# r of blocks 1 to 3 as seven products over pairs of chunks, with a new layout of PSUM

## The chip, the cores and the metric

The kernel runs on one core of one Trainium2 chip. The metric is the device time of one execution in microseconds (us), the median of several runs. A profile of one execution gives every instruction's start and duration on the engines: TensorE (PE, with its weight loads as PEld), VectorE (DVE), ScalarE (ACT), GpSimd (POOL), and SyncE (SP), which issues most DMAs.

## What is computed

One layer over 2048 tokens of 512 channels, all in float32. `xn` is the layer norm of x, and the result is x plus an attention and a feed-forward part:

```python
rvk = einsum('btc,dc->btd', xn, W_rvk)        # 512 -> 3 x 512
r, v, k = split(rvk, 3)
y = sigmoid(r) * wkv(time_decay, time_first, k, v)    # a recurrence over the tokens
attn = einsum('btc,dc->btd', y, W_out)
...
idx = top_k(softmax(xn @ classifier_w.T) + bias, 2)   # of 12: 8 experts, 4 that return x
act = silu(xn @ gate_w[e].T) * (xn @ up_w[e].T)
ffn = sum over the two of weight * (act @ down_w[e].T)
```

## The kernel before

**Tiles.** Channels are cut into 4 chunks of 128, tokens into 4 blocks of 512. A unit is one block and one chunk, 16 units in all, numbered 0 to 15 in order of block and chunk. k, v and r of a unit are 128 channels by 512 tokens. The feed-forward part works on 23 tiles of 128 gathered rows, each with one expert (tiles at places 3 and 7 mix two).

**The products of a unit.** `project` (L273) makes k, v and r of units 0 and 1 plainly: four matmuls of 512 columns each. `seven` (L393) makes units 2 to 15: k and v together are a 2 x 2 block product (halves of the input channels by halves of the tokens), done with seven products in place of eight, by sums of token halves (S1 to S4, `sum_tokens`) and of weights (`wsum`). Each product is two matmuls of 256 columns (L408). Results are added up within PSUM: products 1, 6, 7 and 4 add into one bank in turn and ScalarE copies the sum out after each; 5 and 3 share another bank; 2 has its own. VectorE adds the last parts (`add`, L418); those adds are "owed" and emitted some steps later. r stays plain in `seven`: four matmuls of 512 (L421), and ScalarE takes exp(-r) straight from PSUM (L464). `seven` is a generator of 11 steps.

**The scan of a unit** (`scan`, L296) is the recurrence on VectorE, in five stages: first L307 to L314, then two exponentials on ScalarE (L316, L317), then L323 to L334 (scan steps, and 1 + exp(-r) at L333), then a reciprocal of the first half (L337), then that of the second half and the product y (L340).

**The attention's output** (`attention`, L1012) takes y: a row of 128 tokens is four matmuls of 512 columns (L1040) into a bank `pw`. For rows 0 to 11 VectorE then evicts it with one operation (L1052); rows 12 to 15 are added to rows read back (L1049, L1036).

**A tile of the feed-forward part** is `first_half` (up products into `pg` by `up`, L903, `activate` with ScalarE's tanh at L915 and VectorE at L916 and L917, a gather) and `second_half` (`unite` and `flip`, ScalarE copies for the transposes; `finish` of the tile before, down products into `po`, L851, that ScalarE evicts at L935; fetches).

**PSUM** is eight banks in four pools of two: `ps_mm`, `ps_gu`, `ps_o` and `ps_tr`. `pg` is in `ps_gu`, `po` in `ps_o`, p1 and p3 of `seven` in `ps_mm`, r and p2 in `ps_tr`. Attention rows 0 to 5 take `ps_gu` (even rows) and `ps_o` (odd rows); rows 6 to 11 `ps_o` (even) and `ps_mm` (odd); rows 12 and 13 `ps_o`, 14 and 15 `ps_mm`.

**What sets the order.** Every engine runs its instructions in the order in which the program emits them. The head (norms, transposes, routing) is written out by hand, with `fill(n)` putting n steps of the products between; 50 steps are done there. Behind the head a table (L1094 on) gives every piece of work a due time in a unit of its own and emits the pieces in order of it:

```python
total = groups * 3.43 + TILES * 5.2
one = total / groups / CC                       # a slot: one step or one row's matmul
plan((u - 1) * UNIT + 9 + at, stages[u])        # at = 0, 5, 7.5, 12, 14: five stages of a scan
plan((CC * m + k) * one, group)                 # group m: four steps of products, or a row
plan(CC * (m + 1) * one + 1, group)             # the eviction of that row
plan(4 + spread * i, first_half, i, TILES)      # spread = (total - 12) / TILES
plan(4 + spread * (i + 0.6), second_half, i, TILES)
```

`after` says which groups are rows 0 to 7 of the attention; rows 8 to 15 follow the table. A tile of a pool takes a buffer whose last reader has been emitted, and its first writer waits on the chip until that reader is done.

## Time and profile before

| | us |
|---|---|
| median of 3 runs | 368.78 (368.5 to 370.45) |
| the profiled execution | 368.04, of which its span is 366.3 |
| busy in it: TensorE | 360.8 |
| VectorE | 298.5 |
| ScalarE | 149.0 |
| GpSimd | 88.0 |

The granted TensorE clock is 1.0 throughout. In a line of the timeline the first number is the start in us, the second the duration, then engine, source line, operation, what is written and read, shapes, how many instructions are merged, and in brackets the idle time of the engine before it and what ended it. A float32 matmul leaves two records. [...] The costliest groups of TensorE are the up products (L903, 78.8 us), r (L421, 53.9), the attention's output (L1040, 53.7), the down products (L851, 39.5) and the seven products (L408, four groups of 29.1, 28.9, 28.8 and 14.4).

### The profile page before, as it was taken

The page shows a single profiled execution, that of the slowest core. Times are in us where ns is not written, and L with a number is a line of the kernel's source. Part 1 is how long each engine was busy: PE and PEld are TensorE (multiplying, and loading weights), DVE is VectorE, ACT ScalarE, POOL GpSimd, SP SyncE. Part 2 cuts the span into 40 slices and gives each one's busy share as a digit, 9 for nine tenths or more (in the row PEclk, how much of TensorE's full clock was granted, in tenths as well). Part 3 has the DMA queues.
Part 4 walks back from the last instruction along what each step waited for, and adds up shares of the span by engine and source line. Part 5 has one row for each costly group of instructions (what it writes and reads, how often), then busy time and mean ns, then how long its engine had stood idle before and what let it go on. Part 6 is the DMA issues. An engine that isn't in the chain of part 4 may idle for free. (4 is left out here: it accounts for less than half of the span.)

```text
span 366.3 us, 5027 instructions
## 1 busy us (share of the span) xinstructions
PE 360.8 (99%) x1752; PEld 241.6 (66%) x1752; DVE 298.5 (82%) x508; ACT 149.0 (41%) x267; POOL 88.0 (24%) x120
## 2 busy tenths in 40 slices
PE   8999999999999999999999999999999999999996
PEld 3555468788755686466767777877766787764444
DVE  5888999989998576999597957699969498869971
ACT  2676122345454525255433463435453526332000
POOL 6000200321221232243212214333313222122130
PEclk9999999999999999999999999999999999999999
DMA  7999940886777999979997669999769996924782
GB/s 265 405 350 364 346 145 14 314 262 178 181 218 232 315 332 229 263 152 263 372 361 201 127 204 260 247 234 244 217 208 278 256 244 91 351 41 58 174 137 93
DMA packets 47131, 84.44 MB, mean 231 GB/s; under 512 B 26496, under 2 KB 26880, under 8 KB 43328
## 3 DMA queue, kind: packets, MB, share of 16 engines
q1 hardware_dynamic: 39792, 64.05, 54.9%
q0 software_dynamic: 7312, 20.06, 25.6%
q8 instruction: 14, 0.23, 0.3%
q14 instruction: 13, 0.11, 0.1%
HBM read 63.25 MB, written 19.27 MB: 225 GB/s over the span
## 5 line engine op out<-in xcount | busy, mean ns | idle before, releaser
L903 PEld LDWEIGHTS pg<-xgT,gw 128*128 128x128 f32 x672 | 78.4, 192 | 5.9 <-issue 4.9
L903 PE MATMUL pg<-xgT,gw 128*128 128x128 f32 x672 | 78.8, 275 | 0.2 <-DMA gw<-in_gu_dram 0.2
L939 POOL DMA_INDIRECT out_dram<-yo,to_i x23 | 39.0, 1697 | 149.4 <-DMA out_dram<-yo,to_i 45.6
L337 DVE RECIPROCAL sums<-sums 128x256 f32<-128x256 f32 x32 | 54.6, 1729 | 0.0
L421 PE MATMUL pr<-xnT,wrvk 128*128 128x512 f32 x112 | 53.9, 594 | 0.0
L1040 PE MATMUL pw<-wout_sb,yT 128*128 128x512 f32 x120 | 53.7, 593 | 0.1
L1040 PEld LDWEIGHTS pw<-wout_sb,yT 128*128 128x128 f32 x120 | 22.5, 190 | 26.9 <-issue 26.8
L851 PE MATMUL po<-dw,act 128*128 128x512 f32 x84 | 39.5, 592 | 0.0
L915 ACT ACTIVATE act<-pg 128x256 f32<-128x256 f32 x23 | 8.8, 383 | 69.1 <-PE pg L903 62.6
L916 DVE SCALAR_TENSOR_TENSOR act<-act,pg 128x256 f32<-128x256 f32 x23 | 9.6, 418 | 33.4 <-ACT act L915 33.2
L809 POOL DMA_INDIRECT xg<-xs,token_i x23 | 25.5, 1108 | 46.1 <-DVE empty L760 25.2
L421 PEld LDWEIGHTS pr<-xnT,wrvk 128*128 128x128 f32 x112 | 20.4, 190 | 15.1 <-issue 13.3
L408 PE MATMUL p<-xnT,wrvk 128*128 128x256 f32 x112 | 29.1, 382 | 0.1
L408 PE MATMUL p<-S,wrvk 128*128 128x256 f32 x112 | 28.9, 380 | 0.0
L408 PE MATMUL p<-S,T 128*128 128x256 f32 x112 | 28.8, 379 | 0.0
L323 DVE TENSOR_TENSOR_SCAN sums<-obv,state,a 128x512 f32<-128x512 f32 x16 | 20.5, 1281 | 9.4 <-ACT obv L317 9.3
L408 PEld LDWEIGHTS p<-S,T 128*128 128x128 f32 x112 | 21.0, 190 | 8.7 <-issue 6.2
L851 PEld LDWEIGHTS po<-dw,act 128*128 128x128 f32 x84 | 16.0, 190 | 16.2 <-issue 15.1
L884 ACT COPY xgT<-xq 128x1024 uint16<-128x1024 uint16 x22 | 25.5, 1159 | 0.0
L408 PEld LDWEIGHTS p<-xnT,wrvk 128*128 128x128 f32 x112 | 20.8, 190 | 6.8 <-issue 2.9
L408 PEld LDWEIGHTS p<-S,wrvk 128*128 128x128 f32 x112 | 21.0, 190 | 4.4 <-issue 1.8
L876 ACT COPY xp<-xg 128x1024 uint16<-128x1024 uint16 x22 | 23.0, 1047 | 0.5 <-DMA xg<-xs,token_i 0.5
(224 smaller groups left out, 487.2 us busy)
## 6 DMA issues: line engine op xcount, KB each, us to landing
gw<-in_gu_dram SPq DMA_DIRECT2D x25, 1024.0 KB, 7.9
dw<-in_down_dram SPq DMA_DIRECT2D x25, 512.0 KB, 5.5
x<-in_x_dram SPq DMA_DIRECT2D x16, 256.0 KB, 5.4
xs<-x SPq DMA_DIRECT2D x16, 256.0 KB, 4.4
wrvk<-in_w_rvk_dram SPq DMA_DIRECT2D x3, 1024.0 KB, 8.2
xrow<-xs SPq DMA_DIRECT2D x8, 256.0 KB, 6.4
out_dram<-xrow POOLq DMA_DIRECT2D x8, 256.0 KB, 7.0
xrows<-xs SPq DMA_DIRECT2D x8, 256.0 KB, 7.9
```

What stands on the lines that cost most here:

```text
L323: nc.vector.tensor_tensor_scan(sq, bs, a2, s[:, 3:4], ALU.add, ALU.mult)
L337: nc.vector.reciprocal(den[:, hs], den[:, hs])
L408: nc.tensor.matmul(ps[:, :HALF], w[:, k, cs], a[:, k, :], start=(begin and k == 0), stop=(end and k == 1), skip_group_check=True,)
L421: nc.tensor.matmul(pr, wrvk_sb[0][:, k, cs], xnT[b][:, k, :], start=(k == 0), stop=(k == CC - 1))
L809: nc.gpsimd.indirect_dma_start(out=xg, out_offset=None, in_=xs, in_offset=bass.IndirectOffsetOnAxis(ap=token[:, column(i) : column(i) + 1] ...
L851: nc.tensor.matmul(out_, lhs[:, c, :], rhs[0][:, c, :], start=(c == 0), stop=(c == last))
L876: nc.scalar.copy(xp, st[i]["xg"].bitcast(U16).rearrange("p (c h) -> p h c", h=2))
L884: nc.scalar.copy(xgT.bitcast(U16).rearrange("p c (t h) -> p c t h", h=2), st[i]["xq"].rearrange("p (h c) t -> p c t h", h=2),)
L903: nc.tensor.matmul(pg[:, c // IC, c % IC * P : (c % IC + 1) * P], w[0][:, k, rs], xgT[:, k, :], start=(k == 0), stop=(k == CC - 1),)
L916: nc.vector.scalar_tensor_tensor(act, act, 1.0, pg[:, 0, :], ALU.add, ALU.mult)
L939: nc.gpsimd.indirect_dma_start(out=out, out_offset=bass.IndirectOffsetOnAxis(ap=index, axis=0), in_=yo[ps], in_offset=None, compute_op=ALU ...
L1040: nc.tensor.matmul(po, yT[b][:, c, j * P : (j + 1) * P], wout_sb[:, c, :], start=(c == 0), stop=(c == CC - 1),)
```

## The change

Units 2 and 3 of block 0 still go through `seven`. For blocks 1 to 3 a new generator, `pair`, takes two chunks at once. k and v of each chunk go by the seven products as before (A and B), and r of the two chunks together (R) is now a 2 x 2 block product too, halves of the input channels by halves of the tokens for the two chunks, done with seven products; the token sums are shared with k and v. A pair is 21 steps of one product each in a fixed order. Four sums of r's weights are made, three into new tiles and one in place of the weights: four VectorE operations of 512 elements (`sum_r_weights`), emitted behind the head's last `turn(0)`. exp(-r) is now a ScalarE operation in place, emitted in the scan's third stage. The owed adds carry a clock: each is emitted two steps after its product.

PSUM is laid out anew when the first pair begins (`change_banks`): `ps_o` stays with two buffers; p1 has two, p2, p3, pr (both halves of r's sums) and gu one each. Attention rows 0 to 5 are all in `ps_o`; the later rows that were in `ps_mm` are in p1, the last half row in p3, the rest in `ps_o` as before. The two transposes of mixed tiles (`turn_act`) move from `ps_gu` to `ps_o`.

The plan changes with the number of steps (178 to 172): `groups` 40 to 39, `UNIT` 17.4 to 17.05, rows 4 to 7 one group earlier. The pool of r gets six buffers in place of four, and the memory for the descriptors of GpSimd's DMAs is set to 8192 bytes.

```diff
-    erp = pool("er", 4)
+    erp = pool("er", 6)
...
-    ps_mm = pool("ps_mm", 2, space=bass.MemoryType.PSUM)
-    ps_gu = pool("ps_gu", 2, space=bass.MemoryType.PSUM)
-    ps_o = pool("ps_o", 2, space=bass.MemoryType.PSUM)
-    ps_tr = pool("ps_tr", 2, space=bass.MemoryType.PSUM)
+    ps_o = pool("ps_o", 2, **psum)
+    early = ExitStack()
+    ps_mm, ps_gu, ps_tr = (
+        early.enter_context(tc.tile_pool(name=name, bufs=2, **psum)) for name in ("ps_mm", "ps_gu", "ps_tr")
+    )
+    banks = {}
+
+    def change_banks():
+        early.close()
+        for name, n in (("p1", 2), ("p2", 1), ("p3", 1), ("pr", 1), ("gu", 1)):
+            banks[name] = pool(f"ps_{name}", n, **psum)
...
         er = kvr[b, c, "r"]
+        if b > 0:
+            nc.scalar.activation(er, er, AF.Exp, scale=-1.0)
...
+    def sum_r_weights():
+        for n in (2, 3, 4):
+            rsum[n] = sump.tile([P, 2, 2, P], F32, tag=f"R{n}", name=f"R{n}")
+        nc.vector.tensor_sub(rsum[3], r_weights(1, 1), r_weights(0, 1))
+        nc.vector.tensor_add(rsum[2], rsum[3], r_weights(0, 0))
+        nc.vector.tensor_sub(rsum[4], r_weights(1, 0), rsum[2])
+        rsum[1] = r_weights(0, 1)
+        nc.vector.tensor_sub(rsum[1], r_weights(0, 1), r_weights(0, 0))
...
+        def m1():
+            src = multiply(1)
+            nc.scalar.copy(place(pool_, *k_at, "k")[:, :HALF], src)
...
+        def m2():
+            src = multiply(2)
+            owe(lambda: nc.vector.tensor_add(t["k"][:, :HALF], t["k"][:, :HALF], src))
...
+        def m3():
+            src = multiply(3)
+            nc.scalar.copy(t["more"][:, :HALF], src)
+            owe(lambda: nc.vector.tensor_add(t["v"], t["v"], t["more"]))
...
+    def pair(b, c):
+
+        A, _ = sevens(b, c, False)
+        B, next_sums = sevens(b, c + 1, False)
+        R, _ = sevens(b, c, True)
+        order = "A1 A5 R1 A6 A2 R5 A7 A3 R6 A4 B1 R2 B5 B6 R7 B3 B7 R3 B2 B4 R4".split()
+        done = set()
+        for name in order:
+            while owed and owed[0][0] <= clock[0]:
+                owed.pop(0)[1]()
+            {"A": A, "B": B, "R": R}[name[0]][int(name[1])]()
...
+    def owe(work):
+        owed.append((clock[0] + 2, work))
...
-        for u in range(LEAD, len(units)):
+        for u in range(LEAD, CC):
             yield from seven(*units[u])
+        change_banks()
+        for b in range(1, NTB):
+            for c in range(0, CC, 2):
+                yield from pair(b, c)
...
-            st[i]["pg"] = ps_gu.tile([P, 2, INTER], F32, tag="gu", name=f"pg{i}")
+            st[i]["pg"] = bank("gu", f"pg{i}", (2, INTER))
...
-            if i < (NTB - 2) * NJ - 2 and j % 2 == 0:
-                po = ps_gu.tile([P, C], F32, tag="gu", name=f"pw{i}")
-            elif i < (NTB - 2) * NJ - 2:
-                po = ps_o.tile([P, C], F32, tag="o", name=f"pw{i}")
-            elif j >= 2 if i in orows else j % 2 == 1:
-                po = ps_mm.tile([P, C], F32, tag="mm", name=f"pw{i}")
+            if i >= (NTB - 2) * NJ - 2 and (j >= 2 if i in orows else j % 2 == 1):
+                po = bank("p1", f"pw{i}")
             else:
                 po = ps_o.tile([P, C], F32, tag="o", name=f"pw{i}")
...
-    STEPS = 2 * 3 * CC + 11 * (len(units) - LEAD)
+    STEPS = 2 * 3 * CC + 11 * (CC - LEAD) + 21 * (len(units) - CC) // 2
...
-    UNIT = 17.4
-    after = {10: (0, 0), 11: (0, 1), 16: (0, 2), 17: (0, 3), 30: (1, 0), 31: (1, 1), 38: (1, 2), 39: (1, 3)}
-    groups = (STEPS - DONE) // CC + len(after)
+    UNIT = 17.05
+    after = {10: (0, 0), 11: (0, 1), 16: (0, 2), 17: (0, 3), 29: (1, 0), 30: (1, 1), 37: (1, 2), 38: (1, 3)}
+    groups = -(-(STEPS - DONE) // CC) + len(after)
...
-    nc = bacc.Bacc("TRN2", target_bir_lowering=False, num_devices=1)
+    nc = bacc.Bacc("TRN2", target_bir_lowering=False, num_devices=1, dynamic_dma_scratch_size=8192)
```

More of the change, by code (lines that the diff above doesn't have):

```diff
@@ L82, in layer, with bank @@
     dram = pool("dram", 1, space=bass.MemoryType.DRAM)
-    ps_mm = pool("ps_mm", 2, space=bass.MemoryType.PSUM)
-    ps_gu = pool("ps_gu", 2, space=bass.MemoryType.PSUM)
-    ps_o = pool("ps_o", 2, space=bass.MemoryType.PSUM)
-    ps_tr = pool("ps_tr", 2, space=bass.MemoryType.PSUM)
+    psum = dict(space=bass.MemoryType.PSUM)
+    ps_o = pool("ps_o", 2, **psum)
[8 more added lines that the diff above has]
+            banks[name] = pool(f"ps_{name}", n, **psum)
+    def bank(name, label, shape=(TB,)):
+        return banks[name].tile([P, *shape], F32, tag=name, name=label)
     routing = ExitStack()
@@ L362, in sum_first_weights, with r_weights @@
         nc.vector.tensor_sub(wsum[1], weights(1, 0), weights(2, 0))
+    rsum = {}
+    def r_weights(k, n):
+        both = wrvk_sb[0][:, 2 * k : 2 * k + 2, :].rearrange("p k (q w n) -> p k q w n", q=2, w=2)
+        return both[:, :, :, 1 - n, :]
+    def sum_r_weights():
[6 more added lines that the diff above has]
+        nc.vector.tensor_sub(rsum[1], r_weights(0, 1), r_weights(0, 0))
     def part(b, k, t):
@@ L391, in factors, with r_factors @@
         }[n]()
+    def r_factors(b, n):
+        w = {
+            1: lambda: r_weights(0, 0),
+            2: lambda: r_weights(1, 0),
+            3: lambda: r_weights(1, 1),
+            4: lambda: rsum[4],
+            5: lambda: rsum[1],
+            6: lambda: rsum[2],
+            7: lambda: rsum[3],
+        }[n]()
+        return factors(b, n)[0], w
     def seven(b, c):
@@ L427, in next_sums @@
                 for m in ns:
-                    owed.append(lambda m=m: sum_tokens(b + 1, m))
+                    owe(lambda m=m: sum_tokens(b + 1, m))
         p1 = bank(ps_mm, "mm", "p1_")
@@ L451, in seven @@
         multiply(p2, 2, True, True)
-        owed.append(lambda: add(k[:, :HALF], p2[:, :HALF]))
+        owe(lambda: add(k[:, :HALF], p2[:, :HALF]))
         next_sums((1, 2))
@@ L470, in seven, with sevens, place, at @@
         nc.scalar.copy(more[:, :HALF], p3[:, :HALF])
-        owed.append(lambda: add(v, more))
+        owe(lambda: add(v, more))
         next_sums((4,))
         yield
+    def sevens(b, c, with_r):
+        n = f"{b}_{c}"
+        t, ps = {}, {}
+        def place(pool_, name, c_, role):
+            t[role] = kvr[b, c_, name] = pool_.tile([P, TB], F32, tag=name, name=f"{name}{b}_{c_}")
+            return t[role]
+        def at(m):
+            which = {2: "p2", 3: "p3", 5: "p3"}.get(m, "p1")
+            if with_r and which != "p2":
+                ps.setdefault("pr", None)
+                if ps["pr"] is None:
+                    ps["pr"] = bank("pr", f"pr{n}")
+                h = which == "p3"
+                return ps["pr"][:, h * HALF : (h + 1) * HALF]
+            if m in (1, 2, 5):
+                ps[which] = bank(which, f"{which}{'r' if with_r else ''}_{n}")
+            return ps[which][:, :HALF]
+        def multiply(m):
+            dst = at(m)
+            if with_r:
+                a, w = r_factors(b, m)
+                rows_ = lambda k: w[:, k, c // 2, :]
+            else:
+                a, w = factors(b, m)
+                rows_ = lambda k: w[:, k, c * P : (c + 1) * P]
+            first = m in (1, 2) or (m == 5 and not with_r)
+            for k in range(2):
+                nc.tensor.matmul(
+                    dst,
+                    rows_(k),
+                    a[:, k, :],
+                    start=(first and k == 0),
+                    stop=(k == 1),
+                    skip_group_check=True,
+                )
+            return dst
+        def next_sums(*ns):
+            if c == CC - 1 and b + 1 < NTB:
+                for m in ns:
+                    owe(lambda m=m: sum_tokens(b + 1, m))
+        pool_, k_at, v_at = (erp, ("r", c + 1), ("r", c)) if with_r else (kvp, ("k", c), ("v", c))
+        def m1():
+            src = multiply(1)
+            nc.scalar.copy(place(pool_, *k_at, "k")[:, :HALF], src)
+        def m6():
+            src = multiply(6)
+            nc.scalar.copy(place(pool_, *v_at, "v")[:, :HALF], src)
+        def m5():
+            src = multiply(5)
+            t["more"] = five.tile([P, TB], F32, tag="more", name=f"more{'r' if with_r else ''}{n}")
+            nc.scalar.copy(t["more"][:, HALF:], src)
+        def m2():
+            src = multiply(2)
+            owe(lambda: nc.vector.tensor_add(t["k"][:, :HALF], t["k"][:, :HALF], src))
+        def m7():
+            src = multiply(7)
+            nc.scalar.copy(t["v"][:, HALF:], src)
+        def m4():
+            src = multiply(4)
+            nc.scalar.copy(t["k"][:, HALF:], src)
+        def m3():
+            src = multiply(3)
+            nc.scalar.copy(t["more"][:, :HALF], src)
+            owe(lambda: nc.vector.tensor_add(t["v"], t["v"], t["more"]))
+        return {1: m1, 2: m2, 3: m3, 4: m4, 5: m5, 6: m6, 7: m7}, next_sums
@@ new lines, in pair @@
+    def pair(b, c):
[8 more added lines that the diff above has]
+            {"A": A, "B": B, "R": R}[name[0]][int(name[1])]()
+            done.add(name)
+            for m, users in ((1, "B5 R5"), (2, "B6 R6"), (3, "B7 R7"), (4, "B3 R3")):
+                if name in users and set(users.split()) <= done:
+                    next_sums(m)
+            clock[0] += 1
+            yield
@@ L475, in emit_owed @@
+    clock = [0]
+    def owe(work):
+        owed.append((clock[0] + 2, work))
     def emit_owed(force=False):
         while owed and (force or not head):
-            owed.pop(0)()
+            owed.pop(0)[1]()
     head = True
@@ L503, in emit @@
         for _ in range(n):
-            owed.pop(0)()
+            owed.pop(0)[1]()
     manual = ExitStack()
@@ L864, in turn @@
     def turn(i):
-        pt = ps_tr.tile([P, CC, P], F32, tag="tr", name=f"px{i}")
+        pt = bank("gu", f"px{i}", (CC, P))
         for c in range(CC):
@@ L922, in turn_act @@
     def turn_act(i):
-        pt = ps_gu.tile([P, IC, P], F32, tag="gu", name=f"pa{i}")
+        pt = ps_o.tile([P, IC, P], F32, tag="o", name=f"pa{i}")
         for c in range(IC):
@@ L1024, in attention @@
             if i == NT - 1:
-                for h, ph in enumerate((po, ps_tr.tile([P, C // 2], F32, tag="tr", name="pw_last"))):
+                for h, ph in enumerate((po, bank("p3", "pw_last"))):
                     hs = slice(h * C // 2, (h + 1) * C // 2)
@@ L1085, in layer @@
     turn(0)
+    sum_r_weights()
     DONE = 11 + 9 + 16 + 2 + 12
-    STEPS = 2 * 3 * CC + 11 * (len(units) - LEAD)
-    UNIT = 17.4
-    after = {10: (0, 0), 11: (0, 1), 16: (0, 2), 17: (0, 3), 30: (1, 0), 31: (1, 1), 38: (1, 2), 39: (1, 3)}
-    groups = (STEPS - DONE) // CC + len(after)
+    STEPS = 2 * 3 * CC + 11 * (CC - LEAD) + 21 * (len(units) - CC) // 2
+    UNIT = 17.05
+    after = {10: (0, 0), 11: (0, 1), 16: (0, 2), 17: (0, 3), 29: (1, 0), 30: (1, 1), 37: (1, 2), 38: (1, 3)}
+    groups = -(-(STEPS - DONE) // CC) + len(after)
     total = groups * 3.43 + TILES * 5.2
```

## The prediction

> **What bounds the kernel now.** I read the page's first part (busy shares), then a table of windows, then the timeline of TensorE, and last the timelines of TensorE and VectorE around the rows of the attention.

> ```profile
> PE 360.8 (99%) x1752; PEld 241.6 (66%) x1752; DVE 298.5 (82%) x508; ACT 149.0 (41%) x267; POOL 88.0 (24%) x120
> ```

> ```profile
> 75.00:335.00 260.00, 259.72 (x1333) 184.13 (x1332) 216.03 (x301) 115.56 (x202) 68.70 (x50) 1.00 0.84 229
> ```

> The second line is of the table of windows: from 75 to 335 us TensorE (the second number) is busy 259.72 of 260.00 us, VectorE (the fourth) 216.03. TensorE is the bound, and it waits for nobody there. So products taken away are gained one for one, and every wait put before a product is lost one for one. VectorE has 44 us free, but it works strictly in the written order, and that matters below.

> The price of a product is its distance to the next one (its own duration holds an overlapped end):

> ```profile
> 79.21 1.88 PE L421 MATMUL pr<-xnT,wrvk 128*128 128x512 f32 x4
> 80.93 1.03 PE L408 MATMUL p<-xnT,T 128*128 128x256 f32 x4
> 81.79 1.03 PE L408 MATMUL p<-S,wrvk 128*128 128x256 f32 x4
> 82.66 1.03 PE L408 MATMUL p<-xnT,wrvk 128*128 128x256 f32 x4
> 83.52 1.88 PE L421 MATMUL pr<-xnT,wrvk 128*128 128x512 f32 x4
> ```

> Each matmul leaves two records. Two matmuls of 512 columns take 80.93 - 79.21 = 1.72 us, 0.86 each; three products of two matmuls of 256 columns take 83.52 - 80.93 = 2.59, 0.863 each.

> **Gain.** For a pair of chunks r was 8 matmuls of 512, 8 x 0.859 = 6.87 us; it becomes seven products, 7 x 0.863 = 6.04. Six pairs save 6 x 0.83 = 4.9 us of TensorE.

> **Work that hides.** VectorE gets per pair one add of 256 (0.41 by the k row) and one of 512 (0.67 by the v row), 6.5 us in all, and four weight sums of some 0.68 (the S rows), 2.7: 82% of the span becomes 84.5%. ScalarE loses two exponentials from PSUM (0.60) and gets six copies (0.37) and two exponentials in place (0.63) per pair: +2.3, 13.7 us in all, 41% to 45%. No engine becomes the bound by its sum, so I cost these at nothing except where TensorE waits on them: a copy queued behind xgT, xp and yo held a product up by some 0.25 us at 117.7 in this trace. If such cover failed once in each pair it would be 1.5 us; I take 0. The in-place exponential comes while VectorE does three scan steps (about 4 us) first, and ScalarE is not behind: 0. Halving the descriptor memory of POOL's DMAs could make POOL wait after its five large copies at 36 us; POOL then idles 25.2 us (until `empty`), which covers it. SP's queue gets nothing new.

> **New waits: where an attention row now sits in PSUM.** Before, rows 0 to 5 alternated between `ps_gu` and `ps_o`; now all take `ps_o`, which has two buffers and which every down product `po` needs too. A tile takes a buffer whose last reader is already written in program order, and then waits for that reader on the chip (in this trace po of tile 22 runs at 328.73, before row 6 is evicted at 334.32, so it took the other buffer and not the next in turn). While row j+1 holds one buffer, the next po must take row j's, and that is freed by VectorE's eviction (L1052), behind all that VectorE was given earlier. I follow the new plan: total 39 x 3.43 + 23 x 5.2 = 253.37, a slot 253.37/156 = 1.624, tiles 10.494 apart, scans 17.05 apart.

> Rows 0 and 1. Due: up products of tile 6 at 4 + 6 x 10.494 = 66.97; row 0 until slot 43; scan of unit 4 (due 60.15) third stage 67.65, first reciprocal 72.15; row 0's eviction 44 x 1.624 + 1 = 72.46; po of tile 5 at 4 + 6.6 x 10.494 = 73.26. Row 1 holds its buffer until 78.96. So after tile 6's up products TensorE has two matmuls of row 0 and two of row 1, then po, which needs the eviction; VectorE has act, the third stage, one reciprocal, the eviction. The same stretch before:

> ```profile
> 141.21 3.73 PE L903 MATMUL pg<-xgT,gw 128*128 128x128 f32 x32
> 144.78 3.60 PE L1040 MATMUL pw<-wout_sb,yT 128*128 128x512 f32 x8
> 148.22 1.88 PE L851 MATMUL po<-dw,act 128*128 128x512 f32 x4
> ```

> ```profile
> 145.40 0.42 DVE L916 SCALAR_TENSOR_TENSOR act<-act,pg 128x256 f32<-128x256 f32 x1 [3.13 <-ACT act L915]
> ...
> 151.67 0.74 DVE L1052 SCALAR_TENSOR_TENSOR xrow<-xrow,zw,pw 128x512 f32<-128x512 f32 x1
> 152.33 3.36 DVE L337 RECIPROCAL sums<-sums 128x256 f32<-128x256 f32 x2
> ```

> The eviction ends at 152.33, 7.55 us after the up products (144.78); one reciprocal moves ahead of it (3.36/2 = 1.70), so 9.25. TensorE reaches po after 148.22 - 144.78 = 3.44. It waits 5.8 us. Before, po went at 148.22 without waiting, since row 0 was in `ps_gu`. This one wait costs more than the whole gain.

> Rows 2 and 3. Due: up of tile 10 at 108.94, scan 7's first stage 111.30, row 2's eviction 111.44, po of tile 9 at 115.24 after three matmuls of row 3 (2.58 us). VectorE: act 0.78, first stage 2.66, eviction 0.66 = 4.10 us, by these starts:

> ```profile
> 190.84 0.41 DVE L916 SCALAR_TENSOR_TENSOR act<-act,pg 128x256 f32<-128x256 f32 x1
> ...
> 191.62 0.16 DVE L307 COPY obv<-state 128x3 f32<-128x3 f32 x1
> ...
> 194.28 0.74 DVE L1052 SCALAR_TENSOR_TENSOR xrow<-xrow,zw,pw 128x512 f32<-128x512 f32 x1
> 194.94 0.41 DVE L418 TENSOR_TENSOR k<-k,p 128x256 f32<-128x256 f32 x1
> ```

> It starts 0.62 us after the up products where VectorE is idle (145.40 above), 1.35 us after where it is late, as here (they ended at 189.49). An added v add makes it late again: 4.10 + 1.35 - 2.58 = 2.9 us, at least 2.1.

> Rows 4 and 5. Due: up of tile 18 at 192.90, scan 11's second reciprocal 193.50, eviction 195.90, po of tile 17 at 199.19 after four matmuls. In the trace act of tile 18 starts 0.62 after its up products (277.45 to 278.07) and the eviction ends 3.83 later, after just such a reciprocal: 4.45 - 3.44 = 1.0 us.

> **Start.** Product 5 now comes second and needs S1, which VectorE ends at 70.3 where TensorE is at 69.8; product R5 needs the last of the four new weight sums. VectorE ends S4 at 72.8 and adds 4 x 0.66 = 75.4; TensorE would be there at 73.7: 1.7 us in all, as the first wait is part of it. Price if VectorE were early: 0.

> **End.**

> ```profile
> 318.28 3.73 PE L903 MATMUL pg<-xgT,gw 128*128 128x128 f32 x32
> 321.85 1.02 PE L421 MATMUL pr<-xnT,wrvk 128*128 128x512 f32 x2
> ```

> ```profile
> 347.61 1.40 DVE L1052 SCALAR_TENSOR_TENSOR xrows<-xrows,zw,pw 128x512 f32<-128x512 f32 x2
> ```

> After the last up products (321.85) VectorE needs until 348.27 (half of the last line's pair), 26.4 us, to evict row 8, whose buffer row 12 takes. TensorE came there at 348.9, 0.6 us later. Now one product and not three follow those up products: 0.86 + 24 row matmuls x 0.859 + two po of 1.72 = 24.9 us. VectorE saves 0.2 (a k add for a v add): TensorE waits 26.2 - 24.9 = 1.3, less up to 0.5 because no exponential of r stands ahead of scan 14's. I take 1.0.

> **Clock after a long wait.** The start of this trace shows TensorE slow after idling: in the windows of the warming matmuls 11 of them lie in 4.30 us (1.20 to 5.50), then 12 in 2.20 us (6.30 to 8.50), though the clock column says 1.00 for both. The 26 took 8.3 us; at the later pace (11 starts in 2.20) they take 5.2, 3 less. The 5.8 us wait could bring that back. From below 0: short waits such as that at 117.7 changed no pace. From above 3. The wait lies between an idle start and 0.25 us; I take the middle, 1.5.

> [...]

> **Sum.** -4.9 + 5.8 + 2.9 + 1.0 + 1.7 + 1.0 + 1.5 = +9.0. The profiled execution took 368.04 us (span 366.3), so 377.0; the runs shown have their median 0.7 higher (368.78). I say 377, the kernel slower by some 2.3%.

> **Rivals.** (1) Faster: the evictions come in time. Place: po of tile 5. It decides if row 0 is evicted within 3.4 us of tile 6's up products and not 9.25, or if po finds another buffer. Then the three po waits and the clock go: 368.0 - 4.9 + 1.7 + 1.0 = 365.8, and 363.1 if start and end are covered as well. For it: TensorE is bound elsewhere and VectorE has 16% free. Against: the scan stage stands ahead of the eviction by its due time. Chance 0.13. (2) Half: of the po waits only that of rows 0 and 1 comes, at 4 to 5 us, and the clock holds: 368.0 - 4.9 + 4.5 + 1.7 + 1.0 = 370.3, with the 0.7 of the medians 371, and 368.5 if start and end are covered. It needs VectorE ahead of its dues at the later rows. Chance 0.17. (3) Worse: the clock drops at more than one wait, and copies on ScalarE hold products up (1.5 above): 380 to 383. Chance 0.1. Forecast 0.6 (374 to 380). That r is not multiplied in seven products would show as 512-wide r matmuls in the later blocks; the diff leaves no path to that.

> Less than 0.5% (1.8 us) can't be told from no change. Faster by more than that: rival 1, 0.12. Within (to 370.6): the rest of it and some three fifths of rival 2, 0.11. Slower: 0.77. Range: 369 (most of rival 2) to 382 (most of rival 3), which leaves out 0.19.

> **What would show it.** TensorE idle of some 6 us ahead of po after row 1's second matmul, released by VectorE's L1052 line, and some 3 and 1 us at the next two pairs of rows; R5 late by one or two; the rows of products in the new blocks 0.863 apart. Wrong would be: po without idle there (then rival 1), or the eviction ahead of the scan stage.

## The result and the profile after

The changed kernel takes 379.57 us (median of 6 runs, 378.92 to 381.13), the kernel before 368.29 (median of 6, 367.75 to 370.45): a ratio of 1.0299 [1.0267, 1.0331], 3% slower. The forecast was 377.0 in 369 to 382. So sign and mechanism came as told, and the sum was 2.6 us short.

The profiled execution of the changed kernel took 381.13 us (span 379.3), 13.1 more than that of before (368.04). First the busy shares and the two rows of the page's 40 slices that show TensorE and its granted clock:

```profile
PE 360.8 (95%) x1824; PEld 257.2 (68%) x1824; DVE 306.4 (81%) x524; ACT 160.0 (42%) x303; POOL 91.2 (24%) x120
...
PE   7999999989999999399996999999999899999996
...
PEclk9899999999999999699998999999999999999999
```

TensorE falls from 99% to 95% busy. It has two holes, in slice 17 (about 152 to 161 us, a 3) and in slice 22 (199 to 209, a 6), and in the same two slices the clock row falls to 6 and 8. Its busy time is the same 360.8 us as before although work was taken out: the matmuls that ran at the lower clock were busy for longer (two of `po` took 3.41 us behind the first hole, 1.72 before). A busy share alone would have hidden the gain and the time lost to the lower clock.

The table of waits says whom TensorE waited for (total, number, longest):

```profile
PE po L1002 <- DVE xrow L1199: 9.6, 3, 5.7
```

Three waits of the down product `po` for VectorE's eviction of an attention row (L1199). The timeline of TensorE shows the places:

```profile
148.19 3.60 PE L1187 MATMUL pw<-wout_sb,yT 128*128 128x512 f32 x8
157.52 3.57 PE L1002 MATMUL po<-dw,act 128*128 128x512 f32 x4 [5.73 <-DVE xrow L1199]
160.93 1.88 PE L1187 MATMUL pw<-wout_sb,yT 128*128 128x512 f32 x4
...
200.08 2.74 PE L1187 MATMUL pw<-wout_sb,yT 128*128 128x512 f32 x6
205.68 3.38 PE L1002 MATMUL po<-dw,act 128*128 128x512 f32 x4 [2.86 <-DVE xrow L1199]
208.90 1.02 PE L1187 MATMUL pw<-wout_sb,yT 128*128 128x512 f32 x2
...
291.25 3.60 PE L1187 MATMUL pw<-wout_sb,yT 128*128 128x512 f32 x8
295.84 1.98 PE L1002 MATMUL po<-dw,act 128*128 128x512 f32 x4 [0.99 <-DVE xrow L1199]
```

The eight records before the first `po` hold four matmuls, which at the pitch of 0.859 us end at 148.19 + 3.44 = 151.63; `po` starts at 157.52, 5.9 us later. In the same way the second wait (205.68) is 3.0 us and the third, of tile 17's `po` at 295.84, 1.2. Note also the pitch behind the wait: two `po` matmuls take 160.93 - 157.52 = 3.41 us, where they took 1.72 before; behind the second wait they take 3.22.

What VectorE did ahead of the three evictions stands in its timeline:

```profile
149.60 1.28 DVE L335 TENSOR_TENSOR_SCAN sums<-obv,state,a 128x512 f32<-128x512 f32 x1
...
155.16 1.75 DVE L351 RECIPROCAL sums<-sums 128x256 f32<-128x256 f32 x1
156.82 0.65 DVE L1199 SCALAR_TENSOR_TENSOR xrow<-xrow,zw,pw 128x512 f32<-128x512 f32 x1
...
201.44 0.41 DVE L1067 SCALAR_TENSOR_TENSOR act<-act,pg 128x256 f32<-128x256 f32 x1
...
204.89 0.74 DVE L1199 SCALAR_TENSOR_TENSOR xrow<-xrow,zw,pw 128x512 f32<-128x512 f32 x1
...
292.66 1.74 DVE L351 RECIPROCAL sums<-sums 128x256 f32<-128x256 f32 x1
...
295.04 0.74 DVE L1199 SCALAR_TENSOR_TENSOR xrow<-xrow,zw,pw 128x512 f32<-128x512 f32 x1
```

From 149.60 on it ran a whole scan stage and one reciprocal, as the due times had put them, and only then the 0.65 us eviction that TensorE stood still for. In the second wait it came to tile 10's `act` at 201.44, 1.36 us after the up products ended (at 200.08), and ran the first stage of a scan ahead of the eviction; in the third a reciprocal stood ahead of it.

The table of windows, cut at the edges of the clock's changes, gives the clock by itself (stretch, length, busy us of PE, PEld, DVE, ACT and POOL with counts, granted clock, DMA share, GB/s):

```profile
153.90:160.70 6.80, 3.18 (x4) 1.51 (x5) 6.77 (x8) 0.00 (x0) 0.00 (x0) 0.50 0.39 86
...
205.10:208.50 3.40, 2.82 (x4) 1.26 (x5) 0.53 (x1) 0.00 (x0) 0.94 (x1) 0.50 0.46 79
```

The clock falls to 0.50 some 2.3 us into the first long wait (153.9 against 151.6) and 2.4 us into the second (205.1 against 202.7), stays there to the end of the wait and for a while behind it, and is 1.00 between (160.70 to 205.10). Matmuls fill 3.18 us of the first half-clock stretch and 2.82 of the second. By the pitch there (3.41 us for two matmuls of `po` that took 1.72 before) half of that is lost, an estimate: 1.6 + 1.4 = 3.0 us.

### The profile page after: what moved, and what is told of

It reads as the page before. It is cut to its first block, busy times and chain, and to the rows that moved or that the text cites. A ratio compares the mean times of both kernels' runs of the same rounds, so it can differ in the third digit from the quotient of the medians.

```text
span 379.3 us, 5239 instructions
## 1 busy us (share of the span) xinstructions
PE 360.8 (95%) x1824; PEld 257.2 (68%) x1824; DVE 306.4 (81%) x524; ACT 160.0 (42%) x303; POOL 91.2 (24%) x120
## 4 chain that ended last, share of the span: by engine, by line
PE 74%; DVE 16%; ACT 4%; DMA 3%; issue 2%; SPq 0%; DVEq 0%; ACTq 0%
PE pg L1054 17%; PE p L550 17%; PE po L1002 9%; PE pr L550 7%; PE pw L1187 5%; DVE sums L351 4%; PE p L449 3%; DMA xq<-xp 2%; PE pg L1006 2%; PE pr L291 2%; PE pr L462 2%; PE pk L291 2%; PE pv L291 2%; PE pt L256 2%; DVE sums L337 1%
## 5 line engine op out<-in xcount | busy, mean ns | idle before, releaser
L1090 POOL DMA_INDIRECT out_dram<-yo,to_i x23 | 42.6, 1851 | 154.9 <-ACT yo L1086 47.9
L1002 PE MATMUL po<-dw,act 128*128 128x512 f32 x84 | 42.8, 634 | 9.6 <-DVE xrow L1199 9.6
L1187 PEld LDWEIGHTS pw<-wout_sb,yT 128*128 128x128 f32 x120 | 22.6, 192 | 27.4 <-issue 26.4
L960 POOL DMA_INDIRECT xg<-xs,token_i x23 | 24.3, 1057 | 47.9 <-DVE empty L911 25.2
L1086 ACT ACTIVATE yo<-po,wplace 128x512 f32<-128x512 f32 x23 | 15.8, 688 | 24.2 <-PE po L1002 24.2
L550 PE MATMUL p<-xnT,wrvk 128*128 128x256 f32 x96 | 24.8, 380 | 0.5 <-ACT more L511 0.5
L335 DVE TENSOR_TENSOR_SCAN sums<-obv,state,a 128x512 f32<-128x512 f32 x16 | 20.5, 1281 | 5.6 <-ACT obv L329 5.4
L550 PE MATMUL p<-S,T 128*128 128x256 f32 x96 | 24.8, 381 | 0.0
L550 PE MATMUL p<-S,wrvk 128*128 128x256 f32 x96 | 24.6, 379 | 0.0
L550 PEld LDWEIGHTS p<-S,T 128*128 128x128 f32 x96 | 18.0, 190 | 5.7 <-issue 1.9
L337 DVE TENSOR_TENSOR_SCAN sums<-obv,state,a 128x512 f32<-128x512 f32 x16 | 20.5, 1284 | 0.6
L323 DVE TENSOR_TENSOR_SCAN obv<-wdec,state,k 128x512 f32<-128x512 f32 x16 | 20.4, 1278 | 0.0
L550 PEld LDWEIGHTS p<-xnT,wrvk 128*128 128x128 f32 x96 | 17.8, 190 | 3.9 <-issue 1.0
```

Of the source, the lines that this page charges most:

```text
L335: nc.vector.tensor_tensor_scan(sq, bs, a2, s[:, 3:4], ALU.add, ALU.mult)
L337: nc.vector.tensor_tensor_scan(sp, bvs, a2, s[:, 4:5], ALU.add, ALU.mult)
L550: nc.tensor.matmul(dst, rows_(k), a[:, k, :], start=(first and k == 0), stop=(k == 1), skip_group_check=True,)
L960: nc.gpsimd.indirect_dma_start(out=xg, out_offset=None, in_=xs, in_offset=bass.IndirectOffsetOnAxis(ap=token[:, column(i) : column(i) + 1] ...
L1002: nc.tensor.matmul(out_, lhs[:, c, :], rhs[0][:, c, :], start=(c == 0), stop=(c == last))
L1090: nc.gpsimd.indirect_dma_start(out=out, out_offset=bass.IndirectOffsetOnAxis(ap=index, axis=0), in_=yo[ps], in_offset=None, compute_op=ALU ...
```

## The experiments

The time of before is 368.43 us beside the first four kernels (e1 to e4) and 368.26 beside the others; both are medians of 23 runs.

**e1, the rows alone.** The changed kernel, with the attention rows 0, 2 and 4 taken out of the buffers that `po` uses:

```
             if i >= ...:
                 po = bank("p1", f"pw{i}")
+            elif i < (NTB - 2) * NJ - 2 and j % 2 == 0:
+                po = bank("p1", f"pw{i}")
```

> The changed kernel with attention rows 0, 2 and 4 in p1's two buffers and not in ps_o (rows 1, 3 and 5 stay in ps_o), nothing else. Theory (po waits for a buffer that VectorE frees late): the three idle times of TensorE ahead of po (5.9, 3.0 and 1.2 us in the changed kernel's trace) and the stretches of half clock behind the first two (2.3 and 1.9 us) go, 379.5 - 14.3 = 365 us, clock 1.0 behind the start. Rival (the seven products for r, the thinner buffers of p2, p3 and gu, or VectorE's added work cost the time): the waits turn up at other instructions and the time stays above 376 us.

Measured: 365.93 (365.15 to 368.77, 12 runs), ratio 0.9943 [0.9911, 0.9974]; expected 365, and 376 or more by the rival. One edit of two lines turns 3% slower into 0.6% faster. This is the stretch of the first wait, on TensorE's timeline and in the windows:

```profile
145.58 3.60 PE L1189 MATMUL pw<-wout_sb,yT 128*128 128x512 f32 x8
149.01 1.88 PE L1002 MATMUL po<-dw,act 128*128 128x512 f32 x4
```

```profile
150.00:162.00 12.00, 12.00 (x62) 6.23 (x61) 11.75 (x19) 4.45 (x9) 5.50 (x4) 1.00 0.89 226
```

`po` follows the rows at the plain pitch, TensorE is busy 12.00 of 12.00 us and the clock stays at 1.00, while VectorE (11.75) is as full as ever. So VectorE was never too slow; only the order in which it was asked mattered. The rival that copies on ScalarE hold products up falls here: ScalarE's work is the same as in the changed kernel (159.7 us busy, 160.0 there).

**e2, the start.** e1, with R1 second in the order of products, where product 5 was, and the weight sum for R5 made second of four:

```
-        order = "A1 A5 R1 A6 A2 R5 A7 A3 R6 A4 B1 ...
+        order = "A1 R1 A5 A6 A2 R5 A7 A3 R6 A4 B1 ...
```

> As the kernel with rows 0, 2 and 4 in p1, and besides: a pair's order begins A1 R1 A5 in place of A1 A5 R1, and of the four sums of r's weights the one that R5 needs is made second and not last. Theory (1.2 us of the start is R5 waiting for the fourth sum, and tile 1's up products are 0.8 us late behind it): 1.2 to 2 us less than with the rows alone, 363.0 to 364.0 us. Rival (the start's wait is at the change of PSUM's layout alone): at most 0.6 us less.

Measured: 366.51 (364.87 to 367.48, 12 runs), ratio 0.9946 [0.9927, 0.9964]: a miss, no gain over e1. The two medians are not quite alike: six of these twelve runs and three of e1's have a mean granted clock of 0.995, about what 3.4 us at half clock make of 365 (an estimate: 1.7 of 365 us is 0.5%), and are some 2 us longer (see the last section). Among the others the medians are 365.35 and 365.55, so the gain is 0.2 us and not 1.2. R5's wait is gone, but another has come 30 us later:

```profile
108.12 2.35 PE L1006 MATMUL pg<-gw,xgT 128*32 128x512 f32 x20 [0.85 <-ACT xgT L1035]
```

```profile
105.78 0.63 ACT L328 ACTIVATE a<-a 128x512 f32<-128x512 f32 x1 [1.56 <-DVE a L325]
...
106.92 1.14 ACT L1035 COPY xgT<-xq 128x1024 uint16<-128x1024 uint16 x1
```

The first fence is TensorE: tile 3's up products wait for the copy `xgT`. The second is ScalarE: it stood 1.56 us waiting for VectorE (its exponential needs a row of scan 2), with the copy queued behind. TensorE had come earlier and VectorE had not. By the pitch TensorE waits 1.0 us here and waited 0.1 in e1, so most of the 1.2 us saved at R5 was spent here.

**e3, the eviction earlier.** The changed kernel, with the evictions of rows 0 to 7 due right behind the row's last matmul:

```
-            plan(CC * (m + 1) * one + 1, group)
+            plan((CC * (m + 1) - 1) * one + 0.05, group)
```

> The changed kernel with its banks as they are, but the eviction of rows 0 to 7 due right behind the row's last matmul and not after a slot and one unit more. Theory (VectorE's order decides): row 0's eviction passes one reciprocal (1.7 us), po of tile 5 still waits 4.2 us; row 2's and row 4's evictions pass the scan's first stage and a reciprocal, and the next two waits go: 379.5 - 1.7 - 3.0 - 1.2 - 1.9 = 371.7 us, and 369.5 if 4.2 us of idling leaves the clock alone. Rival (the sharing of the banks costs by itself, whatever VectorE does first): 379 us.

Measured: 373.28 (372.06 to 375.71, 4 runs), ratio 1.0126 [1.0097, 1.0154]; expected 371.7. Of the waits of `po` for the eviction one is left, where the changed kernel has three of 9.6 in sum:

```profile
PE po L1002 <- DVE xrow L1199: 4.2, 1, 4.2
```

```profile
155.30:162.10 6.80, 5.66 (x7) 2.52 (x8) 5.06 (x5) 0.69 (x1) 0.88 (x1) 0.50 0.37 86
```

Those at rows 2 and 4 are gone. That at row 0 is 4.4 by the pitch (VectorE still ran the scan stage ahead of its eviction, but no longer the reciprocal), and the clock fell there once, for 6.8 us of which matmuls filled 5.66: 2.8 us lost. The expectation had left 2.3 for the clock there and taken 1.9 off for the second place, where only 1.4 had been lost; that makes 1.0 of the 1.6 us by which it was short. The terms of this trace are -4.5 + 4.4 + 2.8 + 1.8 (start) + 0.7 (end) = +5.2, and some 2.8 for a stretch at half clock in the head (last section): +8.0, where this execution took 375.71 - 368.04 = 7.7 us more than the profiled one of before. The other three (372.06 to 373.72) have a mean clock of 0.990 to 0.995 and not 0.986, so they spent less time at half clock.

**e4, the wait alone, in the kernel before.** The kernel before, in which only row 0 is put into the buffers of `po`:

```
-            if i < (NTB - 2) * NJ - 2 and j % 2 == 0:
+            if 0 < i < (NTB - 2) * NJ - 2 and j % 2 == 0:
```

> The kernel before, with row 0 of the attention in ps_o and not in ps_gu, nothing else: one wait of the theory by itself. Theory: po of tile 5, which ran at 148.2, waits for row 0's eviction (152.3): 4.1 us of TensorE idle, 368.3 + 4.1 = 372.4 us, and some 374.5 if the clock drops behind it. Rival (where a row lies costs nothing): 368.3 us.

Measured: 376.55 (375.07 to 378.64, 4 runs), ratio 1.0225 [1.0185, 1.0265]: one row in another buffer costs 8.1 us. Its timeline and windows at that place:

```profile
147.00 3.60 PE L1040 MATMUL pw<-wout_sb,yT 128*128 128x512 f32 x8
154.68 3.78 PE L851 MATMUL po<-dw,act 128*128 128x512 f32 x4 [4.08 <-DVE xrow L1052]
```

```profile
154.00:160.90 6.90, 6.22 (x9) 2.94 (x10) 5.29 (x5) 0.69 (x1) 1.44 (x1) 0.51 0.19 53
```

A wait of 154.68 - 150.44 = 4.2 us, then 6.22 us of matmuls at half clock, 3.1 lost: 7.3 us. This execution (377.23) took 9.2 more than the profiled one of before, and some 2.2 of that (row 0 starts at 147.00 us, in the kernel before at 144.78) lies ahead of row 0, with a stretch at half clock in the head, which is not the row's doing. The median of 8.1 lies between two kinds of execution: two of the four have a mean clock of 0.985 or 0.986, the other two of 0.995, which makes some 3.7 us at half clock in all (an estimate: 0.005 of 374 us, doubled), where this trace has some 6.8 at the wait (0.51 over 6.90 us) and some 3.3 in the head (0.50 over the 3.2 us from 10.7 to 13.9, 0.99 over the 6.1 behind them). So the same wait did not cost the same time at half clock each time. From 160.9 to 340 TensorE is busy for 179.10 of 179.10 us again, and nothing is caught up: what was lost at the wait stayed lost. The expectation with the clock (374.5) had 2.1 us for the slow stretch.

**e5, the clock alone.** The changed kernel, with TensorE kept busy through the two long waits by small bf16 matmuls (24 ahead of tile 5's `po`, 12 ahead of tile 9's) whose result nobody reads; the waits stay:

```
+        if i in (5, 9):
+            fill_in = bank("p2", f"fill_in{i}")
+            for _ in range({5: 24, 9: 12}[i]):
+                nc.tensor.matmul(fill_in, ones, ...)
```

> The changed kernel with its two long waits left in, but filled: 24 bf16 matmuls of 512 columns on constant data (5.1 us, into p2's bank, nobody reads them) ahead of po of tile 5, and 12 (2.6 us) ahead of po of tile 9. Extra work of TensorE and nothing removed. Theory (an idle TensorE drops to half clock, which costs 2.3 and 1.9 us behind these two waits): the clock stays 1.0 there and the kernel gets faster by that, 379.5 - 4.2 = 375.3 us. Rival (the slow stretches have another cause, or the waits are priced by themselves): 379.5 us or more.

Measured: 375.81 (375.68 to 377.39, 4 runs), ratio 1.0203 [1.0176, 1.023].

```profile
150.87 5.34 PE L1086 MATMUL fill_in<-ones 128*128 128x512 bf16 x24
156.77 1.98 PE L1002 MATMUL po<-dw,act 128*128 128x512 f32 x4 [0.55 <-DVE xrow L1205]
158.59 1.88 PE L1193 MATMUL pw<-wout_sb,yT 128*128 128x512 f32 x4
```

```profile
150.00:162.00 12.00, 11.45 (x51) 4.53 (x53) 11.50 (x16) 1.22 (x2) 4.54 (x3) 1.00 0.54 139
```

`po` starts 156.77 - 150.87 = 5.9 us after the rows, exactly as late as without the filling, yet the clock is 1.00 here, and likewise from 202 to 209, and the two `po` matmuls take 1.82 us instead of 3.41. Useless work saved 379.57 - 375.81 = 3.8 us (expected 4.2, with 2.3 and 1.9 for the two stretches). 3.0 of it is the half clock counted above. The other 0.8 is about a wait of 0.7 us at 88 us (tile 1's up products for `xgT`) that the profiled execution of the changed kernel has and that of e5 has not; whether all executions differ so wasn't measured.

**e6, the gain alone.** e2, with r of blocks 1 to 3 by eight plain products of 512 again, in the same places of the order, and without its weight sums, copies and in-place exponentials:

```
-        R, _ = sevens(b, c, True)
+        R = {1: r_steps(c, (0,)), 5: r_steps(c, (1,)), ..., 4: r_steps(c + 1, (3,))}
```

> As the kernel with rows 0, 2 and 4 in p1 and the other start, but r of blocks 1 to 3 by eight plain matmuls of 512 columns again, in the places of the seven products of R, with exp from PSUM, and without r's weight sums and adds on VectorE. It prices the seven products alone. Theory: 6 x (8 x 0.859 - 7 x 0.863) = 4.9 us of TensorE come back, less 1 us or so where VectorE, with 9 us less to do, no longer holds TensorE up in the first tiles: 370 to 371 us. Rival (the products save nothing, and the kernels with rows in p1 are faster by their order): 366 us.

Measured: 368.82 (368.41 to 371.21, 12 runs), ratio 1.0013 [0.9989, 1.0037]; expected 370 to 371. Windows of e6:

```profile
70.00:340.00 270.00, 270.00 (x1368) 190.24 (x1367) 222.52 (x311) 118.54 (x209) 69.67 (x52) 1.00 0.83 228
```

TensorE has no gap at all, so e6 lost the wait that e2 had at tile 3, and e2 is the wrong kernel to set it against. Against e8 (below), which has lost that wait too, the seven products of r are worth 368.82 - 364.28 = 4.5 us.

**e7, the descriptor memory alone.** The kernel before, with `dynamic_dma_scratch_size=8192` as its only edit.

> The kernel before with 8192 bytes for the descriptors of GpSimd's DMAs, nothing else. Theory: GpSimd has 25 us to spare after its large copies, no difference, 368.3 us. Rival (fewer descriptors in flight delay gathers and scatters): 370 us or more.

Measured: 368.98 (367.45 to 370.64, 10 runs), ratio 1.0009 [0.9979, 1.0038]. No difference, as expected.

**e8, the exponentials of scan 2 later.** e2, with that group due 0.5 later in the plan's unit, so that ScalarE is given `xgT` first:

```
-            plan((u - 1) * UNIT + 9 + at, stages[u])
+            plan((u - 1) * UNIT + 9 + at + (0.5 if (u, at) == (2, 5) else 0), stages[u])
```

> As the kernel with rows 0, 2 and 4 in p1 and the other start, and the two exponentials of scan 2 due half a unit later, behind the copy of tile 3's transposed rows and not ahead of it. In that kernel's trace the copy stood behind exponentials that waited for VectorE, and tile 3's up products came 1.0 us late. Theory (the start's gain was given back there): 1.0 us less, some 365.3 us. Rival (VectorE is late by itself, and the wait moves on to the next tile): no difference, 366.3 us.

Measured: 364.28 (363.91 to 366.49, 6 runs), ratio 0.9901 [0.9874, 0.9929]: the fastest of all, 1% below the kernel before. Its windows, and ScalarE's timeline:

```profile
70.00:340.00 270.00, 269.95 (x1451) 206.31 (x1452) 234.81 (x332) 129.60 (x245) 73.86 (x53) 1.00 0.87 232
```

```profile
104.25 1.16 ACT L1035 COPY xgT<-xq 128x1024 uint16<-128x1024 uint16 x1
```

The copy now runs at 104.25, ahead of the exponential of scan 2 (106.84), and tile 3's up products start at 107.32, 0.1 late. This confirms e2's reading: the wait was one of order on ScalarE. The medians fell by 2.2 us, but among the runs without the 0.995 clock the median falls from 365.35 to 364.24, by 1.1 us, where 1.0 was expected. TensorE is busy 269.95 of 270.00 us; what is left are 0.6 us ahead of A1 and 0.5 at the end.

## Why the prediction came out as it did

Term by term, predicted against measured in the trace (waits by the pitch of the matmuls):

| step | predicted us | measured us | shown by |
|---|---|---|---|
| seven products for eight | -4.9 | -4.5 | e6 against e8 |
| `po` of tile 5, row 0 | +5.8 | +5.9 | trace; e4, e1 |
| `po` of tile 9, row 2 | +2.9 | +3.0 | trace; e3, e1 |
| `po` of tile 17, row 4 | +1.0 | +1.2 | trace; e3, e1 |
| start | +1.7 | +0.6 and +1.2 | trace; e2 |
| end, row 12 for row 8 | +1.0 | +0.5 | trace |
| slow clock after a long wait | +1.5 | +3.0 | clock row; e5 |
| descriptor memory | 0 | 0 | e7 |

**Right: the three waits.** Following the plan's due times to see what stands ahead of each eviction on VectorE gave each wait within 0.2 us. e4 shows that it is the buffer and not the rest of the change: the same wait comes in the old kernel. e1 shows the other direction. That VectorE had 16% free was no cover, as the forecast held against its first rival: it works in the written order, ran the scan stage from 149.60 us on and the eviction at 156.82, and had its free time elsewhere. The second rival (only one wait, no change of clock) falls by the trace.

**Right: the work that hides.** VectorE is busy for 305.8 us in e1 and ScalarE for 159.7; the forecast's terms make 307.7 (84.0% of the old span, where it wrote 84.5) and 162.7. In e8, where no wait of order is left, TensorE is busy for 269.95 of 270.00 us, so neither engine's added work holds it up. Of the gain, 6 x 0.83 is 5.0 and not 4.9; 4.5 were measured.

**Wrong: the size of the clock term.** The prediction named "the 5.8 us wait" alone, and took the middle of 0 to 3 for it. The measured 3.0 us is the upper end, and comes from two places: 1.6 behind the first wait and 1.4 behind the second, which the term had left out. The clock changes had been priced by the start of the old trace, where the matmuls go at about half pace (11 in 4.30 us, then 12 in 2.20) and the clock column says 1.00. The column is no evidence there: the trace's list of clock changes begins at 6.23 us in that execution, and the column shows 1.00 where the list has nothing. The pace was right, and the value should have lain nearer to the top. The forecast's third rival had the clock drop twice, which came true, and its 380 to 383 begins just above the median; but its other half, copies queued on ScalarE that hold products up, is not seen. The one place like it (0.7 us at 88 us) waits for a copy that had itself waited 0.75 us for a DMA.

The list of clock changes of the changed kernel's execution gives the lengths: the clock is 0.50 from 10.55 to 13.96 us, from 153.91 to 160.74 and from 205.11 to 208.52, which is 3.41, 6.83 and 3.41 us. These are the 3.41 us ahead of the falls at the two waits, and those behind the first:

```profile
150.50:153.91 3.41, 1.29 (x4) 0.22 (x2) 3.23 (x7) 0.79 (x1) 2.80 (x2) 1.00 0.60 154
153.91:157.32 3.41, 0.00 (x0) 0.00 (x0) 3.41 (x4) 0.00 (x0) 0.00 (x0) 0.50 0.78 171
201.70:205.11 3.41, 1.12 (x3) 0.19 (x1) 3.34 (x7) 0.96 (x2) 0.00 (x0) 1.00 1.20 238
```

TensorE was busy for 1.29 and 1.12 us of the 3.41 ahead of the falls, about a third, and the second wait, of 3.0 us, was enough: 1.4 us were lost there, for which the forecast had nothing.

**Right in size, wrong in place: the start.** The sum of 1.7 was measured as 1.8, but the first part was another wait, so that the sums agree is luck. This is A1 and R5 on TensorE's timeline, the last weight sum on VectorE's, and an exponential on ScalarE's:

```profile
71.45 1.13 PE L550 MATMUL p<-xnT,wrvk 128*128 128x256 f32 x4 [0.46 <-ACT more L511]
...
77.48 1.10 PE L550 MATMUL pr<-S,wrvk 128*128 128x256 f32 x4 [1.00 <-ACT obv L329]
```

```profile
76.64 0.68 DVE L391 TENSOR_TENSOR wrvk<-wrvk 128x512 f32<-128x512 f32 x1
```

```profile
76.71 0.62 ACT L329 ACTIVATE obv<-obv 128x512 f32<-128x512 f32 x1
```

A1 itself, at 71.45, waited 0.6 us for a ScalarE copy that still read a PSUM buffer of the head: the new layout of PSUM behind the head, which the prediction had not gone through buffer by buffer. That wait covered the one for S1. R5 waited 1.2 us. The bracket puts it down to `obv` on ScalarE, which ends at 76.71 + 0.62 = 77.33; the last weight sum (L391) ends at 76.64 + 0.68 = 77.32. The times can't decide between the two, but e2 does. There R5 starts at the plain pitch, ahead of that exponential, since its own weight sum now comes earlier and has ended at 74.44:

```profile
73.89 1.03 PE L550 MATMUL p<-xnT,wrvk 128*128 128x256 f32 x4
74.75 1.03 PE L550 MATMUL pr<-S,wrvk 128*128 128x256 f32 x4
```

```profile
75.16 0.62 ACT L329 ACTIVATE obv<-obv 128x512 f32<-128x512 f32 x1
```

So R5 doesn't need `obv`: where two candidates end together, the name in brackets can be the wrong one.

**Half right: the end.** 0.5 for 1.0:

```profile
359.59 1.95 PE L1187 MATMUL pw<-wout_sb,yT 128*128 128x512 f32 x4
361.89 10.54 PE L1187 MATMUL pw<-wout_sb,yT 128*128 128x512 f32 x24 [0.35 <-DVE xrows L1199]
```

The term was the small difference of two long stretches (26.2 and 24.9 us, less some), so half a microsecond either way was to be expected. The 0.5 stays in e1, e6 and e8, so it doesn't come from the rows 0 to 4.

The sum of the measured terms is -4.5 + 5.9 + 3.0 + 1.2 + 1.8 + 0.5 + 3.0 = +10.9 us; the medians differ by 11.3, and the 0.7 us wait at 88 us is not in the sum. The profiled executions differ by 13.1; that of the changed kernel has besides a stretch at half clock in the head, which costs it some 1.9 us (last section), and with both the terms make +13.5. Without the row waits and the slow clock they give -4.5 + 1.8 + 0.5 = -2.2, and e1 measured -2.5.

Two things stay open. How busy TensorE must be for the clock to stay at 1.00 was not shown (last section). And 0.6 us at A1 was not removed by any kernel here.

## What to carry to other kernels

Before two tiles share a buffer, look at when the reader of each gets its turn in the written order of its engine: a tile whose eviction stands behind a scan stage (5.6 us here, 149.60 to 155.16) must not hold the buffer that the bounding engine needs next, however much free time the evicting engine has in sum. Price a wait of TensorE with what the clock does at it: here those of 3.0 to 5.9 us cost 1.4 to 3.1 us besides their length, at a granted clock of 0.50 (it varied between executions of one kernel), those of 1.2 us and less their length alone, and where other matmuls filled the wait (e5) the clock was 1.00. A gain at the bound is only kept if the next late thing is moved too: here the gain of 4.5 us was worth 2.5, and then 4.0, as the waits behind it were taken away.

## What the runs showed of the hardware

The wait of 4.2 us had more time at half clock than that of 3.0. In the changed kernel's second stretch TensorE was busy for 2.84 of the first 3.41 us (205.11 to 208.52), and the clock was 1.00 behind them. In e4, where the clock fell at about 154.0 us, it was busy from 154.68 on, some 2.7 of the first 3.4 us, and in e3, where it fell at about 155.3, from 156.44 on, some 2.3, and the clock was at half for about as long again. What made the difference was not shown.

In the profiled execution of the changed kernel the clock is at half for a further 3.41 us in the head (10.55 to 13.96 us). In those of e4, e5 and e7 it is 0.50 from 10.7 to 13.9, and in that of e3 0.70 there and 0.88 from 13.9 to 20; in those of before and of e1, e2, e6 and e8 it is 1.00 in both. The same product behind it (`p<-xnT,T` near 68 us) starts at 69.10 us in the changed kernel and at 69.18 in e5, and between 67.05 and 67.48 in before, e1, e6 and e8; row 0 starts at 147.00 in e4 and at 144.78 before, and at 148.64 in e3 and 145.58 in e1. So the executions with the stretch come some 2 to 3 us later out of the head. The same kernel can have it or not: one run of e5 took 377.39 us at a mean clock of 0.995, and its others 375.68 to 375.92 at 1.0. It is one reason why the times of one kernel spread over 2 to 3 us; differences of a microsecond were therefore read from the pitch of the matmuls, not from the times.

Ahead of this fall TensorE was busy for 1.84 of 3.41 us (7.14 to 10.55) in the changed kernel; in the kernel before, where the clock stays at 1.00, for 3.14 of the same 3.41. The last products of the kernel before fill 1.57 of 3.41 us (361.21 to 364.62), and the clock was 1.00 to the end of the span, so the busy time alone does not tell the two apart. Why TensorE idles more in the head of some executions was not followed.
